# Cross attention beside the feed-forward products: tiles' scores every three slots, values two slots later, output products and third norms three slots later

## The chip, the core and the metric

The kernel runs on one core of a Trainium2 chip. The core has five engines, each with a queue of its own that it works off in order: TensorE (PE; its weight loads are shown apart as PEld), VectorE (DVE), ScalarE (ACT), GpSimd (POOL) and SyncE (SP), which here issues the DMAs. Engines wait for each other through semaphores. Matmuls write into eight banks of PSUM, from which VectorE and ScalarE read. The metric is the device time of one execution in microseconds (us); several executions are timed, and one more is recorded by the profiler.

## The reference

A transformer of one encoder layer (77 rows of context, two sequences) and one decoder layer (2 x 2048 rows, width 512, 16 heads of 32, feed-forward width 2048), in float32. Biases of scores depend on the relative position only. The decoder's part:

```python
y = y + _mha(yn, yn, dec_sa_in_w, dec_sa_in_b, dec_sa_out_w, dec_sa_out_b, sb)
y = y + _mha(_ln(y, dec_n2_s, dec_n2_b), memory, dec_ca_in_w, dec_ca_in_b, dec_ca_out_w, dec_ca_out_b, cb)
h = _ln(y, dec_n3_s, dec_n3_b)
y = y + (jax.nn.relu(h @ dec_ff1_w.T + dec_ff1_b) @ dec_ff2_w.T + dec_ff2_b)
```

`_mha` projects queries from its first argument and keys and values from its second, takes softmax(q k / sqrt(32) + bias) times v by heads, and multiplies by the output weights. In the cross attention (`ca`) the keys are the 77 rows that the encoder made, so each query row has 16 x 77 probabilities.

## The kernel before

The 4096 decoder rows are eight blocks of 512 rows (`blocks`), each of four tiles of 128 rows. The encoder, the self attention of all blocks and the cross attention of the first block come first. The last part, lines 2000 to 2006, is the one around the change: for each block x it runs the feed-forward part of block x in `per` = 56 slots, and beside it the cross attention of block x + 1, which `cross` (line 1747) deals out over the same slots.

A slot is `next(side)`, which issues all functions of `cross` planned for that slot, and then `ff_slot` (line 1724). Instructions go to each engine in exactly this order: the schedule is written by hand. Large products are built in Strassen's manner (Winograd's form): seven products of sums of quarters instead of eight. Hence the sums on VectorE and GpSimd and the lists `ONE` and `TWO` of which product uses which sums.

**Feed-forward slots.** Slots 0 to 27 (`first_product`, line 1649; matmuls at line 1658): hidden = first weights times norm, twice seven products in two slots each. The result goes out of PSUM by a copy on ScalarE (L1668), by an add on VectorE (L1671), by both ReLU activations on ScalarE (L1674), or by several of these, depending on the product. Products accumulate in banks 4 to 7, so a product waits until what is read from its bank has been read. Slots 28 to 55 (`second_product`, line 1678; matmuls at line 1687): seven products of seven parts each; a product takes four slots with 2, 2, 2 and 1 parts. Results are mixed at L1695 to L1703 and added to the rows at L1707 on GpSimd. The left operands of product j are sums made by `sums_h` (line 1615) in slots 24 + 4j to 27 + 4j: half sums on VectorE (L1607) and quarter sums at L1625 and, through the helper `minus`, L965, on VectorE and GpSimd. For j = 0 they are a sum on VectorE in slot 24, one on GpSimd in slot 25, one on VectorE in slot 26, one on GpSimd in slot 27; part 2 of the product, the first of slot 29, multiplies the one of slot 25.

**Side slots.** Per block and tile t:

- slots 0 to 7: second norm (`norm_stages`, line 785: statistics, centering, turning by TensorE with activations at L814); slots 11 to 14 add a row on GpSimd (L806);
- slots 9 to 12: queries (`q_product`, matmuls L1773);
- `SCORE_AT[t]` + 0, 2, 3, 3, 6: scores (L839; then L848 and L849 on VectorE, which take maxima from PSUM and subtract them, with an added bias at L846 for two tiles of the one block that starts the second sequence), exponential on ScalarE (L852), sums and reciprocal on VectorE (L857, L858), normalizing on GpSimd (L863), turning of 32 x 32 blocks on VectorE (`blocks_turned`, L1804). The scores of one tile fill all of banks 0 to 3;
- `VALUES_AT` + g, g = 0 to 3: probabilities times values (`times_v`, matmuls L1815) into banks 0 to 3, for all four tiles at once, so the first of them needs all four turned tiles. With the last group, `values_out` (line 1823) copies the results out (L1827) and makes sums of them for the output products (L965, L1833);
- `OUT_AT`: two sets of seven output products (`o_product`, matmuls L1854), four slots each, added to the rows at L1858;
- `NORM_AT[t]` + 0, 2, 4: the third norm, of which the turned tile goes to `nTt`. The feed-forward part of the next block reads it from its slot 0 on (sums of it on GpSimd in slots 0, 1, 4 and 6, L965).

Functions planned for one slot are issued in the order in which `cross` appended them, for the tiles by t: turning of an earlier tile, then sums and normalizing of the next one, then scores of the one after.

Weights come in tiles of 256 KB through a ring of places. `weight_tiles` (line 1532) lists them in the order of use: in each slot first those of the side stage (`cross_tiles`, line 1521, which follows `Q_SLOTS` and `O_SLOTS`), then those of the feed-forward product. `feed` (line 1559) is called in each slot and issues as many loads on SP as places have come free.

Of the kernel before, what the change touches and what calls it, by code (L numbers as in the profile page):

```python
# [54 lines left out]
def tile_encoder_decoder(ctx: ExitStack, tc: tile.TileContext, ins, out):  # L55
# [103 lines left out]
    with (  # L159
# [625 lines left out]
        def norm_stages(y, n, row, place, done):  # L785

            keep = {}

            def stats():
                st = sm.tile([P, 6], F32, name="bnst", tag="bnst")  # L790
                mv = sm.tile([P, 2], F32, name="cmv", tag="cmv", bufs=4)
                rs = sm.tile([P, 3], F32, name="crs", tag="crs", bufs=4)
                nc.vector.bn_stats(st, y())
                nc.vector.bn_aggr(mv, st)
                nc.vector.tensor_scalar_add(rs[:, 0:1], mv[:, 1:2], EPS)
                nc.gpsimd.tensor_tensor(rs[:, 1:2], rs[:, 0:1], mhalf[:, 0:1], ALU.pow)
                nc.gpsimd.tensor_scalar(rs[:, 2:3], mv[:, 0:1], rs[:, 1:2], -1.0, ALU.mult, ALU.mult)
                keep.update(rs=rs)

            def center():  # L800
                xn = keep["xn"] = place()
                rs = keep["rs"]
                nc.scalar.activation(xn, y(), AF.Identity, bias=rs[:, 2:3], scale=rs[:, 1:2])

            def add():
                nc.gpsimd.tensor_tensor(y(), y(), row, ALU.add)  # L806

            def turned():
                xn, pt, dst = keep["xn"], bank(), done()
                for c in range(NC):  # L810
                    nc.tensor.transpose(pt[:, ts(c, P)], xn[:, ts(c, P)], ident)  # L811
                for c in range(NC):
                    sc, bi = vec(f"dec_{n}_s", c), vec(f"dec_{n}_b", c)
                    nc.scalar.activation(dst[:, c, :], pt[:, ts(c, P)], AF.Identity, bias=bi, scale=sc)  # L814

            return stats, center, turned, add
# [543 lines left out]
        def y_of(x, t):  # L1360
            return ys[x % 3][:, t, :]
# [150 lines left out]
            return ins["dec_ff1_wT"][c * TOK : (c + 1) * TOK, o : o + TOK].rearrange("(c p) o -> p c o", p=P)  # L1512

        Q_SLOTS = {9: (0, 1), 10: (2, 3), 11: (4, 5), 12: (6,)}
        SCORE_AT = (13, 17, 21, 25)
        VALUES_AT = 32
        OUT_AT = (37, 41)
        NORM_AT = (41, 42, 45, 46)
        O_SLOTS = {at + k: js for at in OUT_AT for k, js in enumerate(((0, 1), (2, 3), (4, 5), (6,)))}

        def cross_tiles(n):
# [225 lines left out]
        def cross(x):  # L1747
# [58 lines left out]
            def times_v(g):  # L1806
                if g == 0:
                    for _ in range(P // RB):
                        bank()
                pT = prs.rearrange("p t (h c q) -> p t h c q", h=H, c=KC)  # L1810
                for c in range(KC):
                    for a in range(P // RB):
                        for r in range(HC):
                            h = g * HC + r
                            nc.tensor.matmul(  # L1815
                                psum[rows4(r), a, ts(g, P)], v4[ts(a, RB), c, ts(h, HD)],
                                pT[ts(a, RB), :, h, c, :], start=(c == 0), stop=(c == KC - 1),
                            )
# [24 lines left out]
            def o_product(t, j):  # L1843
                if j == 0:
                    held["out"] = bank(), bank()
                name, by, chain, fresh, to = ONE[j]
                a, mm = of_o(t, name), held["out"][chain][:, :TOK]
                if by[0] == "T":
                    w = next_w(2)
                else:  # L1850
                    r, c = int(by[0]) - 1, int(by[1]) - 1
                    w = wbt[:, 2 * r : 2 * r + 2, ts(c, TOK)]
                for c in range(2):
                    nc.tensor.matmul(  # L1854
                        mm, a[:, ts(c, P)], w[:, c, :], start=fresh and c == 0, stop=c == 1, skip_group_check=True
                    )
                d = y_of(x, t + int(to[0]) - 1)[:, ts(int(to[1]) - 1, TOK)]
                ve.tensor_tensor(d, d, mm, ALU.add)  # L1858
# [3 lines left out]
            for n, js in O_SLOTS.items():  # L1862
                t = 0 if n < OUT_AT[1] else 2
                plan[n].append(lambda t=t, js=js: [o_product(t, j) for j in js])
# [12 lines left out]
            for g in range(NC):  # L1877
                plan[VALUES_AT + g].append(lambda g=g: times_v(g))
            plan[VALUES_AT + NC - 1].append(values_out)
            for t in range(TB):  # L1880
                at = SCORE_AT[t]
                y = lambda t=t: y_of(x, t)
# [7 lines left out]
                fs = norm_stages(y, "n3", bo, next_xt, lambda t=t: nTt[:, :, ts(t, P)])  # L1890
                at = NORM_AT[t]
                for k, f in zip((0, 2, 4), fs):
# [151 lines left out]
```

## Time and profile before

| | us |
|---|---|
| runs (3): median, lowest, highest | 2768.71, 2766.49, 2769.78 |
| profiled execution, its own time | 2766.32 |
| its span, first to last instruction | 2764.5 |
| TensorE busy | 2685.6 |
| VectorE busy | 1906.8 |
| ScalarE busy | 1474.9 |
| GpSimd busy | 997.9 |

The last part of the kernel, in which the slots of eight blocks run, lies between about 1680 and 2764 us of the span; one block of 56 slots with its side stage takes 142 us. Views of the profile that follow: the head of the page (span; busy time, share and instructions of each engine); the list of waits (who waited for whom: total us, times, longest us); the timeline (start in us, duration, engine, line and operation, output and inputs, count; in brackets the idle time before it and what ended it); and windows (from:to, length, busy time and count of PE, PEld, DVE, ACT and POOL, then the granted TensorE clock as a share of full speed, the busy share of the DMA engines, and GB/s). Rows of the timeline that stand one behind another are merged instructions of one line; matmuls are pipelined, and their ends are modelled, so ends can overlap the next start.

### The profile page before, as it was taken

The page shows a single profiled execution, that of the slowest core. Times are in us where ns is not written, and L with a number is a line of the kernel's source. Part 1 is how long each engine was busy: PE and PEld are TensorE (multiplying, and loading weights), DVE is VectorE, ACT ScalarE, POOL GpSimd, SP SyncE. Part 2 cuts the span into 40 slices and gives each one's busy share as a digit, 9 for nine tenths or more (in the row PEclk, how much of TensorE's full clock was granted, in tenths as well). Part 3 has the DMA queues.
Part 4 walks back from the last instruction along what each step waited for, and adds up shares of the span by engine and source line. Part 5 has one row for each costly group of instructions (what it writes and reads, how often), then busy time and mean ns, then how long its engine had stood idle before and what let it go on. Part 6 is the DMA issues. An engine that isn't in the chain of part 4 may idle for free.

```text
span 2764.5 us, 70789 instructions
## 1 busy us (share of the span) xinstructions
PE 2685.6 (97%) x27950; PEld 2192.0 (79%) x27950; DVE 1906.8 (69%) x5473; ACT 1474.9 (53%) x2866; POOL 997.9 (36%) x845
## 2 busy tenths in 40 slices
PE   9999999999999999999999999898989898989898
PEld 5678777787776677777787787888879797979798
DVE  4776688888884677778888874747474747474745
ACT  3555567777886566667777774242414242424231
POOL 2612145401201404223200112645454555555445
PEclk9999999999999999999999999999999999999999
DMA  8734355411215413333211234666657565657476
GB/s 238 214 90 143 118 167 171 137 52 44 74 33 124 128 57 94 110 115 127 87 52 38 67 111 152 195 182 187 188 179 225 158 209 163 214 158 218 135 228 206
DMA packets 296893, 386.20 MB, mean 140 GB/s; under 512 B 41330, under 2 KB 165794, under 8 KB 296434
## 3 DMA queue, kind: packets, MB, share of 16 engines
q1 hardware_dynamic: 296562, 381.68, 46.2%
q8 instruction: 221, 3.62, 0.6%
q14 instruction: 110, 0.90, 0.1%
HBM read 335.10 MB, written 46.47 MB: 138 GB/s over the span
## 4 chain that ended last, share of the span: by engine, by line
PE 83%; DVE 10%; ACT 3%; issue 2%; POOL 1%; DMA 1%; SPq 0%; DVEq 0%; ACTq 0%; POOLq 0%
PE psum L427 18%; PE psum L375 11%; PE psum L1687 10%; PE psum L1658 9%; PE psum L456 9%; PE psum L1137 8%; PE psum L1773 3%; PE psum L1854 3%; PE psum L1052 2%; PE psum L1815 2%; DVE pp L849 1%; DVE cmx L848 1%; DVE csu L857 1%; PE psum L590 1%; PE psum L811 1%
## 5 line engine op out<-in xcount | busy, mean ns | idle before, releaser
L406 ACT ACTIVATE pp<-pp,nm 128x128 f32<-128x128 f32 (+15 forms) x512 | 611.8, 1200 | 29.4 <-DVE nm L401 28.6
L384 DVE TENSOR_SCALAR_CACHE_REDUCE pp<-psum 128x512 f32<-128x512 f32 (+3 forms) x1024 | 556.1, 590 | 51.2 <-PE psum L375 49.7
L434 ACT COPY pts<-psum 128x512 f32<-128x512 f32 x714 | 384.1, 594 | 311.2 <-PE psum L427 263.3
L427 PE MATMUL psum<-ident,pp 128*128 128x128 f32 x4352 | 527.4, 276 | 4.6 <-ACT nT L310 4.0
L427 PEld LDWEIGHTS psum<-ident,pp 128*128 128x128 f32 x4352 | 471.3, 141 | 55.1 <-DVE pp L384 21.6
L375 PE MATMUL psum<-kT,q 32*128 32x512 f32 (+3 forms) x2560 | 336.8, 559 | 4.1 <-ACT kT L231 1.4
L456 PEld LDWEIGHTS psum<-pts,vv 128*32 128x32 f32 x8704 | 226.4, 110 | 127.3 <-DVE pp L384 55.4
L432 DVE COPY pts<-psum 128x512 f32<-128x512 f32 x374 | 245.2, 686 | 81.5 <-PE psum L427 79.3
L456 PE MATMUL psum<-pts,vv 128*32 128x128 f32 x8704 | 279.4, 275 | 0.7 <-DVE mx L391 0.3
L965 POOL TENSOR_TENSOR pp<-pp 128x512 f32<-128x512 f32 x159 | 206.8, 1321 | 107.4 <-DMA pp<-in_dec_ff_wT_dram 50.9
L375 PEld LDWEIGHTS psum<-kT,q 32*128 32x128 f32 x2560 | 146.5, 184 | 109.0 <-issue 41.1
L391 DVE CUSTOM_DVE_ANT_0 pp<-psum,bias 128x256 f32<-128x256 f32 (+1 forms) x512 | 195.9, 411 | 19.7 <-PE psum L375 19.7
L1687 PE MATMUL psum<-oT,pp 128*128 128x128 f32 x1544 | 193.6, 280 | 0.4 <-POOL pp L965 0.4
L1687 PEld LDWEIGHTS psum<-oT,pp 128*128 128x128 f32 x1544 | 186.3, 195 | 6.2 <-issue 3.5
L1674 ACT ACTIVATE kT<-kT,vecs 128x256 f32<-128x256 f32 x192 | 87.1, 500 | 194.9 <-DVE kT L1671 194.2
L1695 ACT COPY pts<-psum 128x128 f32<-128x128 f32 x56 | 15.1, 269 | 307.9 <-PE psum L1687 307.9
L863 POOL TENSOR_TENSOR pp<-pp,cri 128x1232 f32<-128x1232 f32 x32 | 75.6, 2363 | 272.9 <-DVE cri L858 248.7
L1671 DVE TENSOR_TENSOR kT<-kT,psum 128x512 f32<-128x512 f32 x96 | 65.4, 681 | 153.9 <-PE psum L1658 153.7
L494 POOL TENSOR_TENSOR oT<-rirows,oT 128x512 f32<-128x512 f32 x30 | 38.4, 1278 | 294.9 <-DMA rirows<-rec 169.4
L1658 PE MATMUL psum<-vv,oT 128*128 128x256 f32 x600 | 138.2, 381 | 0.0
L1687 PE MATMUL psum<-pp 128*128 128x128 f32 x1016 | 132.4, 284 | 1.8 <-POOL pp L965 1.2
L1687 PEld LDWEIGHTS psum<-pp 128*128 128x128 f32 x1016 | 126.1, 199 | 6.8 <-issue 2.7
(287 smaller groups left out, 4583.4 us busy)
## 6 DMA issues: line engine op xcount, KB each, us to landing
oT<-w_d SPq DMA_DIRECT2D x311, 256.0 KB
pp<-w_d SPq DMA_DIRECT2D x209, 256.0 KB
bias<-tzg SPq DMA_DIRECT2D x128, 128.0 KB
pp<-in_dec_ff_wT_dram SPq DMA_DIRECT2D x63, 256.0 KB
wqk<-in_dec_sa_in_wT_dram SPq DMA_DIRECT2D x52, 256.0 KB
oT<-in_dec_ff_wT_dram SPq DMA_DIRECT2D x49, 256.0 KB
wqk<-sa_q SPq DMA_DIRECT2D x84, 128.0 KB
oT<-wo_d SPq DMA_DIRECT2D x34, 256.0 KB
```

What stands on the lines that cost most here:

```text
L375: nc.tensor.matmul(banks[r][:, : kn * P], q[rows4(r), ts(t, P)], kT[rows4(r), g, k0 * P : (k0 + kn) * P], start=True, stop=True,)
L384: nc.vector.tensor_scalar(p[:, k0 : k0 + far], s[:, :far], 1.0, None, ALU.mult, ALU.max, accum_out=st["mx"][:, r, c : c + 1],)
L391: nc.vector.tensor_tensor_reduce(p[:, k0 + far : i + 1], s[:, far:kn], near[:, 2 - (kn - far) :], 1.0, LOWEST, ALU.add, ALU.max, accum_out ...
L406: nc.scalar.activation(p, p, AF.Exp, bias=nm, accum_out=to)
L427: nc.tensor.transpose(pt[:, ts(x, P)], state[n]["p"][r][:, k], ident)
L432: nc.vector.tensor_copy(pts[:, : len(load), :], pt[:, :w])
L434: nc.scalar.copy(pts[:, : len(load), :], pt[:, :w])
L456: nc.tensor.matmul(ot[rows4(r)], vv[:, k, ts(g * HC + r, HD)], got.pop((n, k, r)), start=k == k0 and (whole or not begun), stop=k == k1 - ...
L965: engine.tensor_tensor(out, a, b, ALU.subtract)
L1137: nc.tensor.matmul(mm[:, ts(f, TOK)], left[:, c, ts(f, P)], right[:, c, :], start=c == 0, stop=c == 1,)
L1658: nc.tensor.matmul(mm[:, ts(f, TOK)], a[:, c, ts(f, P)], b[:, c, :], start=fresh and f == 0 and c == 0, stop=c == 1, skip_group_check=True,)
L1687: nc.tensor.matmul(psum[:, bank_i, ts(col, P)], lhs[:, c, :], w[:, c, :], start=fresh and k in (0, 3) and c == 0, stop=c == 3, skip_group_ ...
```

## The change

Four constants change, and with them, through `O_SLOTS`, the slots of the output products and the place of their weight tiles in the order of loads.

```diff
-        SCORE_AT = (13, 17, 21, 25)
-        VALUES_AT = 32
-        OUT_AT = (37, 41)
-        NORM_AT = (41, 42, 45, 46)
+        SCORE_AT = (13, 16, 19, 22)
+        VALUES_AT = 34
+        OUT_AT = (40, 44)
+        NORM_AT = (44, 45, 48, 49)
         O_SLOTS = {at + k: js for at in OUT_AT for k, js in enumerate(((0, 1), (2, 3), (4, 5), (6,)))}
```

The slots of the side stage in both versions:

| | before | after |
|---|---|---|
| scores of tiles 0 to 3 | 13, 17, 21, 25 | 13, 16, 19, 22 |
| exponentials | 15, 19, 23, 27 | 15, 18, 21, 24 |
| sums, normalizing | 16, 20, 24, 28 | 16, 19, 22, 25 |
| blocks turned | 19, 23, 27, 31 | 19, 22, 25, 28 |
| values | 32 to 35 | 34 to 37 |
| output products | 37 to 40, 41 to 44 | 40 to 43, 44 to 47 |
| third norm, first and last step | 41, 42, 45, 46 and 45, 46, 49, 50 | 44, 45, 48, 49 and 48, 49, 52, 53 |

## The prediction

> **What bounds the kernel now.** I read the head of the page, then TensorE's waits in the stretch from 1600 to 2764 us (seven blocks of 56 slots in which a side stage, the cross attention of the next block, runs between the feed-forward products of this one), then the timelines of one block on TensorE and VectorE, then the granted clock.
>
> ```profile
> span 2764.5 us, 70789 instructions
> PE 2685.6 (97%) x27950; PEld 2192.0 (79%) x27950; DVE 1906.8 (69%) x5473; ACT 1474.9 (53%) x2866; POOL 997.9 (36%) x845
> ```
> ```profile
> PE psum L1815 <- DVE pp L1804: 42.7, 7, 7.9
> PE psum L1854 <- DVE pts L1833: 9.1, 7, 1.3
> PE psum L1854 <- DVE vv L1858: 3.4, 7, 0.5
> ```
>
> TensorE is the bound (97% of the span), and in this stretch it waits at three places only, once per block each: 42.7 us for the last turned tile of probabilities (L1804) ahead of the first value product (L1815), 9.1 us for the sums of the values (L1833) ahead of the output product (L1854), 3.4 us inside that product. Here is one block on TensorE (start, duration, count, idle time before):
>
> ```profile
> 2274.92 1.13 PE L839 MATMUL psum<-pts,bias 32*128 32x77 f32 x32
> ...
> 2277.81 5.34 PE L1658 MATMUL psum<-nT,oT 128*128 128x256 f32 x24
> ...
> 2311.12 1.06 PE L1687 MATMUL psum<-oT,kT 128*128 128x128 f32 x8
> 2317.99 2.17 PE L1815 MATMUL psum<-pp,pts 32*32 32x128 f32 x96 [5.81 <-DVE pp L1804]
> 2320.09 3.78 PE L1687 MATMUL psum<-oT,pp 128*128 128x128 f32 x16
> 2323.80 1.56 PE L1815 MATMUL psum<-pp,pts 32*32 32x128 f32 x96
> 2325.29 2.05 PE L1687 MATMUL psum<-pp 128*128 128x128 f32 x16
> ```
>
> I count time from 2274.92, where the first tile's scores start in slot 13. A score costs 1.06 to 1.1, a slot of first products 1.73 (5.34 for three, ends overlapping), a slot of second products of 16 matmuls 1.78 and of 8 matmuls 0.89. Slots 13 to 31 are four scores, 15 first-product slots and one set of four second-product slots (6.24): 36.4. TensorE is through with them at 37.3 (2312.18), so it has lost 0.9 in all on the way, and then stands still for 5.81.
>
> Behind that stall the same work takes longer: 2.17 for a value group that takes 1.56 two rows on, 3.78 for products that take 2.05. The clock says why:
>
> ```profile
> 1740.50:1746.30 5.80, 0.02 (x1) 0.00 (x0) 5.80 (x6) 0.00 (x0) 5.10 (x4) 0.78 0.90 314
> 2595.30:2601.10 5.80, 0.09 (x1) 0.00 (x0) 5.80 (x6) 0.00 (x0) 5.10 (x4) 0.95 0.43 154
> 2312.20:2317.20 5.00, 0.00 (x0) 0.00 (x0) 5.00 (x5) 0.00 (x0) 4.30 (x3) 1.00 1.01 358
> 2170.40:2176.20 5.80, 0.00 (x0) 0.00 (x0) 5.80 (x6) 0.00 (x0) 5.10 (x4) 0.50 0.53 201
> 1746.30:1753.30 7.00, 6.98 (x212) 6.00 (x213) 4.65 (x6) 0.00 (x0) 6.22 (x5) 0.70 0.30 91
> 2601.10:2608.10 7.00, 6.91 (x186) 6.03 (x192) 4.72 (x7) 0.00 (x0) 6.23 (x5) 0.56 0.13 41
> ```
>
> The third figure from the right is the granted clock. It falls to 0.50 during each of the seven stalls and stays there for a while. The last two rows are the first and last of the seven 7 us behind a stall; their shortfall, 7 x (1 - clock) over all seven, sums to 17.6 us: 2.5 per block. So the stall and what hangs on it cost 42.7 + 17.6, the two smaller waits 12.5. The block that reads bias tiles (it scores from 2129.10) comes to its stall 2.0 later than the others do. Together 74.8 us can be won at most.
>
> What holds TensorE is VectorE's queue:
>
> ```profile
> 2276.07 0.48 DVE L848 TENSOR_REDUCE cmx<-psum 128x4 f32<-128x308 f32 x1 [3.80 <-PE psum L839]
> ...
> 2279.29 0.48 DVE L849 TENSOR_TENSOR pp<-psum,cmx 128x308 f32<-128x308 f32 x1
> 2281.50 1.44 DVE L857 TENSOR_REDUCE csu<-pp 128x16 f32<-128x1232 f32 x1 [1.74 <-ACT pp L852]
> ...
> 2283.19 0.69 DVE L1671 TENSOR_TENSOR kT<-kT,psum 128x512 f32<-128x512 f32 x1
> ...
> 2287.85 0.68 DVE L1671 TENSOR_TENSOR kT<-kT,psum 128x512 f32<-128x512 f32 x1
> 2288.44 1.77 DVE L1804 STREAM_TRANSPOSE pp<-pp 128x1536 f32<-128x1536 f32 x1
> ...
> 2310.68 3.89 DVE L1607 TENSOR_TENSOR pp<-kT 128x512 f32<-128x512 f32 x3
> ...
> 2316.17 1.76 DVE L1804 STREAM_TRANSPOSE pp<-pp 128x1536 f32<-128x1536 f32 x1
> ```
>
> Per tile: scores S 3.6 to 3.7, sums U 1.65 (L857, L858), turn X 1.7, and for the products an add of 0.6 (L1671, start to start 0.59). Tile t's are S0 to S3 and so on. The last turn X3 stands behind four half sums (L1607) of the second products.
>
> **The change, part by part.** No instruction is added or removed. Scores move 0, 1, 2, 3 slots earlier, values and their turns' deadline 2 later, output products 3 later. The other rows that the new queue needs:
>
> ```profile
> 2288.56 0.91 ACT L1674 ACTIVATE kT<-kT,vecs 128x256 f32<-128x256 f32 x2 [3.74 <-DVE kT L1671]
> 2289.84 1.25 ACT L852 ACTIVATE pp<-pp 128x1232 f32<-128x1232 f32 x1
> ```
> ```profile
> 2301.32 2.27 POOL L863 TENSOR_TENSOR pp<-pp,cri 128x1232 f32<-128x1232 f32 x1 [6.06 <-DVE cri L858]
> 2303.54 1.26 POOL L965 TENSOR_TENSOR pp<-pp,kT 128x512 f32<-128x512 f32 x1
> ```
>
> VectorE's new order, with ends: S0 4.85; U0 waits for its exponential as now, 8.3; S1 (slot 16) 11.9; adds of slots 16 and 17, 13.1; X0 14.8; exponential 1 stands on ScalarE behind the two activations that wait for the adds (0.9 each, then 1.25), so it ends at 15.5, and U1 at 17.2; S2 (slot 19) 20.8; X1 22.5; U2 24.1; S3 27.7; adds of 22 and 23, half sum (0.55), add of 24: 30.1; X2 31.8; U3 33.4. Then GpSimd: normalizing tile 3 (L863, N3) to 35.9, and the next sum (L965) to 37.2.
>
> That last step is the new wait. N3 moves from slot 28 to slot 25, where the side stage's functions are issued ahead of the feed-forward ones. So it passes the sums that the first second-product takes from GpSimd (issued in slots 25 and 27), which now queue behind it. TensorE's slot 29 multiplies the first of them.
>
> TensorE: tile 3's scores come at 19.1 in slot 22 and need all four banks, which S2 frees at 20.8: wait 1.7. Slot 29 comes at 32.0 + 0.7 (most of its lag as now) + 1.7 = 34.4 and waits to 37.2: 2.8. After that slot 32 begins at 41.7; its second left operand is the fourth half sum, behind N3 (35.9), X3 (1.7), two half sums (1.3 and 0.7 to 1.3), one more (1.3), a short add and itself (1.3): 42.5 to 43.1, needed at 42.6. Values in slot 34, at 45.3, find X3 done since 37.6. So 4.5 of new waits per block, 31.5 in seven, and 4.3 more in the block with bias tiles, by the same walk with its longer scores, worked out from these rows:
>
> ```profile
> 2130.24 0.48 DVE L846 TENSOR_TENSOR pp<-psum,pp 128x308 f32<-128x308 f32 x1 [3.80 <-PE psum L839]
> ...
> 2135.52 0.48 DVE L849 TENSOR_TENSOR pp<-pp,cmx 128x308 f32<-128x308 f32 x1
> ```
>
> Together 35.8. The outputs and the norms:
>
> ```profile
> 2333.85 0.42 DVE L965 TENSOR_TENSOR wqk<-xr,psum 128x256 f32<-128x256 f32 x1 [6.05 <-ACT pts L1827]
> ...
> 2335.77 0.41 DVE L1833 TENSOR_TENSOR pts<-psum,pts 128x256 f32<-128x256 f32 x1
> 2371.72 1.50 ACT L814 ACTIVATE nT<-psum,vecs 128x128 f32<-128x128 f32 x4 [0.57 <-PE psum L811]
> 2383.91 1.27 POOL L965 TENSOR_TENSOR vv<-nT 128x512 f32<-128x512 f32 x1
> ```
>
> From the last value group (ends 2332.2) to the end of its sums (2336.2) are 4.0. TensorE has 2.67 of products for that now and 4.45 after (slots 37 to 39), so the 9.1 go; the 3.4 sit behind half sums that meet the product elsewhere, and I count them gone (if not, 3 us less). The third norm's last activations end at 2373.2, their first reader on GpSimd starts at 2383.9; three slots later takes at most 4.5 of these 10.7, so this costs nothing. Eight weight tiles of the output product enter SP's queue three slots later, in the order in which they are used; no wait above is for a DMA, so I price that at nothing, at worst a few tenths per block.
>
> Left is the clock after the new waits. By the seven stalls it halved 2.1 to 5.3 us after TensorE went idle (a row of length L and clock c halved 2 x L x (1 - c) before its end: 3.2 and 5.2 for the first and the last of the seven, which are quoted; in the 0.50 row idle time began at 2168.34, so 2.1; in the 5.00 us row not yet). That looks like fixed windows, each judged at its end by its idle share. A wait of 1.7 is shorter than any of these. For 2.8, four of the seven phases (2.1, 2.9, 3.0, 3.2 us) would have halved it, three (5.0 to 5.3) not. I take four, and one more for the bias block's longer waits, at 2.5 each as now: 12.5. Bounds: none, or all nine: 0 to 22.5.
>
> Sum: 74.8 - 35.8 - 12.5 = 26.5 us less. The profiled execution took 2766.3; the median shown, 2768.7, is 2.4 above it, and 2768.7 - 26.5 = 2742.
>
> **Rivals.** (a) The clock needs a whole idle window to fall, so no new wait costs clock: 39.0 less, 2730. The Trainium skill, "TensorE: Matmul & The Clock Gate", Part 1, has this rule: half clock after at least one idle window of about 3.4 us. By that rule 2.8 us could never do it; the trace speaks against it, with 0.50 granted 2.1 us after idle time began. Chance 0.20.
> (b) No new wait arises: VectorE's lag is smaller than worked out, or the sums come in time. All 74.8 go but for the score waits (up to 12): about 2700. Against it: VectorE has the same work and idles only some 2.6 in the new order up to U3. Chance 0.08.
> (c) Both new waits cost clock in every block, 16 x 2.5 = 40: nothing is left, 2768 to 2770. Against it: 1.7 is under the shortest 2.1. Chance 0.07.
> (d) Slower: exponentials late on ScalarE. Each stands behind activations that wait for VectorE's adds; if U1, U2 and U3 each idle 1.8 as U0 does, the sum behind N3 comes 4.6 later. It decides from 3.8 later (26.5 / 7). Price: 39.0 - 7 x 4.6 - 10 x 2.5 = 18 us longer, 2787. Against it: U2 and U3 find VectorE behind, not ahead. Chance 0.05.
>
> **How the numbers follow.** My forecast has 0.60; its own range is no cold clock with VectorE 1 us per block earlier (2722) to all nine with 1 us later (2759). It contains (a). (b), (c), (d) and a little of the edges lie outside: range 2720 to 2758. A measurement of this kernel can tell 0.2%, 5.5 us, from no change. Faster by more: forecast, (a), (b) and a bit of (c), 0.90; within, the rest of (c), 0.05; slower, (d), 0.05.
>
> **What would show it.** Right: no wait of L1815 for L1804; per block a wait of L839 for L849 of about 1.7 and one of L1687 for GpSimd's L965 (behind L863) of about 2.8, in slot 29; no wait of L1854 for L1833; granted clock under 1 behind some of the waits, not all. Wrong: the wait of L1687 absent, or longer than 4, or new waits at the start of a block (first readers of the third norm).

## The result and the profile after

| | before | after |
|---|---|---|
| median of 20 runs (us) | 2768.49 | 2761.84 |
| lowest and highest | 2763.96, 2771.78 | 2754.05, 2770.9 |
| profiled execution, its own time | 2766.32 | 2757.55 |
| its span | 2764.5 | 2755.8 |

The ratio is 0.9975, with a 95% interval of 0.9966 to 0.9984: faster by a quarter of a per cent, 6.65 us. Forecast were 26.5 us and 2742, with a range of 2720 to 2758. The direction was right; the time lies above the range.

TensorE's waits in the seven blocks of the changed kernel (who waited for whom, total us, times, longest), 1600 to 2755 us of the span:

```profile
PE psum L1687 <- POOL pp L965: 23.7, 9, 3.2
PE psum L1815 <- issue: 8.1, 8, 1.9
PE psum L839 <- DVE pp L849: 2.8, 6, 0.5
PE psum L839 <- DVE pp L846: 2.0, 2, 1.0
PE psum L1687 <- issue: 1.9, 2, 1.3
PE psum L1854 <- DVE vv L1858: 1.1, 7, 0.2
```

The 42.7 us of L1815 for L1804 and the 9.1 of L1854 for L1833 are gone. In their place stands the forecast wait of L1687 for GpSimd's L965, and one that was not forecast: 10 us "issue", in which the profile shows nothing that TensorE waits for. Here is the same block as in the prediction, TensorE's timeline from its first score at 2270.41:

```profile
2289.72 0.91 PE L839 MATMUL psum<-pts,bias 32*128 32x77 f32 x6
2291.09 1.11 PE L839 MATMUL psum<-pts,bias 32*128 32x77 f32 x26 [0.46 <-DVE pp L849]
...
2307.69 1.16 PE L1687 MATMUL psum<-pp 128*128 128x128 f32 x8 [3.15 <-POOL pp L965]
2308.68 4.47 PE L1687 MATMUL psum<-oT,pp 128*128 128x128 f32 x24
...
2317.55 1.49 PE L1815 MATMUL psum<-pp,pts 32*32 32x128 f32 x96
2318.97 2.05 PE L1687 MATMUL psum<-pp 128*128 128x128 f32 x16
2320.95 1.49 PE L1815 MATMUL psum<-pp,pts 32*32 32x128 f32 x96
2322.36 0.49 PE L1687 MATMUL psum<-oT,pp 128*128 128x128 f32 x2
2324.19 0.83 PE L1687 MATMUL psum<-oT,pp 128*128 128x128 f32 x6 [1.33 <-issue]
```

Tile 3's scores take 2.41 instead of 1.06 (2289.72 to 2292.13), slot 29 waits 3.15, 24 matmuls behind it take 4.47 instead of 2.84, and in slot 35 TensorE stops after two of eight matmuls of one weight tile, whose operands are all there. The windows (busy times, then granted clock, busy share of the DMA engines, GB/s) put the clock and the DMA engines beside this; first two of the changed kernel, then two of the kernel before around its old stall:

```profile
2309.13:2312.54 3.41, 3.41 (x18) 3.41 (x18) 3.28 (x5) 0.02 (x1) 2.25 (x2) 0.52 0.56 178
2317.60:2322.40 4.80, 4.80 (x210) 4.08 (x209) 2.90 (x4) 0.00 (x0) 4.03 (x4) 1.00 1.02 337
```
```profile
2312.20:2318.00 5.80, 0.01 (x2) 0.01 (x2) 5.80 (x6) 0.00 (x0) 5.10 (x4) 0.93 0.94 334
2318.00:2324.00 6.00, 6.00 (x128) 5.22 (x144) 4.63 (x6) 0.00 (x0) 5.22 (x5) 0.50 0.08 28
```

Before, the DMA engines did their backlog (0.94) while TensorE stood still, and were nearly idle (0.08) when the value products began. After, the value products begin while they are full (1.02). It is alike in all seven blocks: in the first 6 us of value products the DMA engines are busy 0.08 to 0.22 before and 0.73 to 1.00 after.

### The profile page after: what moved, and what is told of

Its sections match the earlier page's. It is cut to its first block, busy times and chain, and to the rows that moved or that the text cites. A ratio compares the mean times of both kernels' runs of the same rounds, so it can differ in the third digit from the quotient of the medians.

```text
span 2755.8 us, 70838 instructions
## 1 busy us (share of the span) xinstructions
PE 2696.6 (98%) x27950; PEld 2198.3 (80%) x27950; DVE 1918.2 (70%) x5473; ACT 1473.2 (53%) x2866; POOL 1005.9 (37%) x845
## 3 DMA queue, kind: packets, MB, share of 16 engines
q8 instruction: 221, 3.62, 0.5%
## 4 chain that ended last, share of the span: by engine, by line
PE 82%; DVE 8%; issue 3%; ACT 3%; POOL 2%; DMA 1%; SPq 1%; DVEq 0%; POOLq 0%; ACTq 0%
PE psum L427 18%; PE psum L1687 11%; PE psum L375 11%; PE psum L456 9%; PE psum L1658 9%; PE psum L1137 8%; PE psum L1773 3%; PE psum L1854 3%; PE psum L1052 2%; PE psum L1815 2%; DVE csu L857 1%; DVE pp L849 1%; DVE cmx L848 1%; PE psum L811 1%; ACT pp L406 1%
## 5 line engine op out<-in xcount | busy, mean ns | idle before, releaser
L965 POOL TENSOR_TENSOR pp<-pp 128x512 f32<-128x512 f32 x159 | 212.1, 1357 | 111.7 <-DMA pp<-in_dec_ff_wT_dram 50.8
L1687 PE MATMUL psum<-oT,pp 128*128 128x128 f32 x1544 | 199.1, 284 | 18.2 <-POOL pp L965 16.2
L1687 PEld LDWEIGHTS psum<-oT,pp 128*128 128x128 f32 x1544 | 190.8, 199 | 25.2 <-POOL pp L965 17.4
L1687 PE MATMUL psum<-pp 128*128 128x128 f32 x1016 | 128.3, 280 | 7.7 <-POOL pp L965 7.5
L1687 PEld LDWEIGHTS psum<-pp 128*128 128x128 f32 x1016 | 123.1, 195 | 11.6 <-POOL pp L965 8.2
```

The lines of the kernel that those rows point to most:

```text
L965: engine.tensor_tensor(out, a, b, ALU.subtract)
L1687: nc.tensor.matmul(psum[:, bank_i, ts(col, P)], lhs[:, c, :], w[:, c, :], start=fresh and k in (0, 3) and c == 0, stop=c == 3, skip_group_ ...
```

## The experiments

e1 to e4, e5 to e8, and e9 with e10 ran on three chips. Each time is a median, and each ratio is to the kernel before on the same chip (medians 2766.55, 2767.67 and 2768.60), so medians of different groups may be some 2 us apart for that alone.

| run | edit against | us | ratio (95%) |
|---|---|---|---|
| the change | before | 2761.84 | 0.9975 (0.9966 to 0.9984) |
| e1 | the change: tile 3's normalizing back in slot 28 | 2733.15 | 0.9876 (0.9863 to 0.9889) |
| e2 | the change: idle time of slot 29 filled | 2750.53 | 0.9944 (0.9932 to 0.9956) |
| e3 | the change: rows loaded in slots 16 to 19 | 2750.49 | 0.9938 (0.9927 to 0.9950) |
| e4 | the change: old slots of scores | 2737.47 | 0.9895 (0.9882 to 0.9908) |
| e5 | the change: only its slots of scores | 2764.74 | 0.9989 (0.9978 to 0.9999) |
| e6 | e1 and e3 together | 2720.24 | 0.9827 (0.9814 to 0.9841) |
| e7 | e4 and e3 together | 2734.43 | 0.9879 (0.9866 to 0.9893) |
| e8 | e6, fourth tile's scores in slot 23 | 2720.80 | 0.9827 (0.9813 to 0.9840) |
| e9 | e6 and four idle copies of 256 KB in slots 28 to 31 | 2734.13 | 0.9880 (0.9866 to 0.9895) |
| e10 | e6 and eight such copies | 2758.29 | 0.9967 (0.9953 to 0.9981) |

The theory at the start: what is left sits in the wait behind tile 3's normalizing and in the clock behind that wait. The rival: the DMA engines, which had caught up during the old stall, are now the limit, and give back whatever is freed.

**e1, the order on GpSimd.**

```diff
-                for k, f in zip((0, 2, 3, 3, 6), fs):
+                for k, f in zip((0, 2, 3, 6, 9) if t == 3 else (0, 2, 3, 3, 6), fs):
```

> The changed kernel with only tile 3's normalizing (L863) in slot 28 and its turn (L1804) in slot 31, as before the change, so that GpSimd's sums of slots 25 and 27 stand ahead of it. If what is left is the wait of L1687 for GpSimd (22 us in seven blocks) and the cold clock behind it (7 x 1.7 = 12): 2728 to 2738, no wait of L1687 for L965 on GpSimd over 0.5. If the DMA engines are the limit there (they are at 1.0 from slot 32 on, and TensorE stops inside value products for nothing the profile shows): the time comes back as longer stops in L1815 and L1687, 2750 to 2760.

Measured 2733.15, inside the first range. In its list of waits (1680 to 2680 us) the one for GpSimd is gone, and the unnamed ones have grown:

```profile
PE psum L1815 <- issue: 12.1, 9, 2.7
PE psum L839 <- DVE pp L849: 4.5, 10, 0.7
PE psum L839 <- DVE pp L846: 2.0, 2, 1.0
PE psum L1687 <- DVE pp L965: 1.5, 6, 0.3
```

So the first theory holds for some 27 to 29 us (28.7 by medians, 26.8 with each kernel against its own kernel before), and the rival for a rest.

**e2, the clock.** 24 transposes, not read by anyone, stand ahead of slot 29's products.

```diff
+            if x + 1 < len(blocks) and (j, part) == (0, 1):
+                for _ in range(24):
+                    nc.tensor.transpose(psum[:, 0, :P], ident, ident)
```

> The changed kernel with 24 transposes of the identity into bank 0 (about 2.6 us, their result is not read) ahead of the products of slot 29, in the time in which TensorE waits for GpSimd. If the clock falls by the idle share of a window, the idle time of 0.6 left cannot lower it: granted clock 1.00 behind slot 29 in all seven blocks, 7 x 1.7 = 12 us less than the changed kernel, 2748 to 2753. If the stops for the DMA engines take the place, as TensorE is then earlier at slot 32: 2757 to 2762.

Measured 2750.53, 11.3 less than the changed kernel by medians, 9.4 less with each against its own kernel before. In its timeline (line numbers three higher here) the transposes take 2.8 of the idle time; the window row below it has the clock at 1.00, and it does not fall behind slot 29 in any of the seven blocks:

```profile
2308.62 2.78 PE L1685 MATMUL psum<-ident 128*128 128x128 f32 x24
2311.95 1.16 PE L1690 MATMUL psum<-pp 128*128 128x128 f32 x8 [0.54 <-POOL pp L965]
```
```profile
2311.40:2318.00 6.60, 6.06 (x55) 6.06 (x55) 6.52 (x10) 0.27 (x1) 5.22 (x5) 1.00 0.58 157
```

Work that does nothing shortened the kernel. The halved clock behind slot 29 is thereby shown as a cost of its own.

**e3, the traffic in slots 28 to 31.**

```diff
-            if FIRST <= n < FIRST + TB:
-                new_y(x + 2, n - FIRST)
+            if 16 <= n < 16 + TB:
+                new_y(x + 2, n - 16)
```

> The changed kernel with the loads of the next rows (4 x 256 KB, new_y) issued in slots 16 to 19 instead of 28 to 31. If TensorE's stops inside the value products (10 us in seven blocks, for nothing the profile shows) come from full DMA engines, they shrink to under 3 and the time falls by 5 to 8, to 2754 to 2757. If they are TensorE's own limit on short matmuls, they stay at 8 to 10 and the time at 2760 to 2763.

Measured 2750.49, more than expected (11.35 less than the changed kernel); the stops in the value products fell as expected, those of L1687 hardly:

```profile
PE psum L1687 <- POOL pp L965: 22.1, 7, 3.2
PE psum L839 <- DVE pp L849: 3.6, 8, 0.5
PE psum L1815 <- issue: 2.5, 6, 0.8
PE psum L839 <- DVE pp L846: 2.0, 2, 1.0
PE psum L1687 <- issue: 1.7, 2, 1.2
```

Between the two profiled executions the difference is 7.1 (2757.55 and 2750.49); the rest is that the changed kernel's profiled run lay 4.3 under its median, and e3's at its own.

**e4 and e5, one half of the change each.** e4 has the old `SCORE_AT` with the new `VALUES_AT`, `OUT_AT` and `NORM_AT`, e5 the reverse.

> The old slots of scores (13, 17, 21, 25) with the new ones of values, outputs and norms. Worked out from the old trace: the wait ahead of the values (5.8) becomes one of 3.1 in slot 32 for VectorE's fourth half sum (L1607, done at 41.3 after the first score, needed at 38.2), the waits for L1833 and L1858 (12.5) go, the clock falls in four to seven blocks. If the earlier scores brought little and the later values and outputs the gain: 2755 to 2763, as the changed kernel or better. If the earlier scores matter: 2764 to 2768.

> The new slots of scores (13, 16, 19, 22) with the old ones of values, outputs and norms. By the traces so far: the wait ahead of the values (5.8 and its clock) goes, the waits of L1839 for banks, of L1687 for the sum behind tile 3's normalizing (3.1) and its clock come, and the 9 to 12 us ahead of and in the output products stay: 2758 to 2766. If the earlier scores are what shortened the changed kernel: 2750 to 2756.

(L1839 there stands for L839.) Measured 2737.47 and 2764.74. e4 beats the changed kernel by far, which was not expected. The wait in slot 32 came nearly as worked out (2.5 for 3.1), unnamed in the profile, but TensorE goes on as soon as the third of VectorE's half sums is through (2298.05), not the fourth:

```profile
2298.15 3.56 PE L1687 MATMUL psum<-oT,pp 128*128 128x128 f32 x16 [2.49 <-issue]
```
```profile
2294.15 3.90 DVE L1607 TENSOR_TENSOR pp<-kT 128x512 f32<-128x512 f32 x3
```

The gain is that e4 stops only 3.0 us in value products and has not the scores' wait for banks; its wait in slot 32 stands in place of the 3.15 in slot 29. In e5 the 22.1 for GpSimd stands beside the 9.1 for L1833, as expected:

```profile
PE psum L1687 <- POOL pp L965: 22.1, 7, 3.2
PE psum L1854 <- DVE pts L1833: 9.1, 7, 1.3
```

So the later values and outputs alone are worth 29 us, the earlier scores alone 3, both together 6.65: the earlier scores, as they were placed, take 22 back.

**e6, e7, e8.** e6 joins e1 and e3, e7 joins e4 and e3. Tile 3 is normalized in slot 28 and turned in slot 31 in both, so they differ in the slots of the scores and of what hangs on them (exponentials, sums, the first three tiles' normalizing and turns).

> Both at once: tile 3's normalizing behind the sums (2733 by itself) and the rows loaded in slots 16 to 19. In the former run TensorE stopped 12 us inside value products for nothing the profile shows, with full DMA engines. If that is the cause there too, 8 to 12 less: 2721 to 2726. If the rows were late for another reason, 2731 to 2735.

> Old slots of scores, new ones of values, outputs and norms (2737 by itself), and the rows loaded in slots 16 to 19. That kernel stopped only some 3 us inside value products, so 0 to 4 less: 2733 to 2738. A gain of 8 or more as in the changed kernel would say that the loads in slots 28 to 31 cost something beside those stops.

> As e6, with the fourth tile's scores in slot 23, its sums in 26, its normalizing in 28 and turn in 31. The scores of slot 22 lose 1.3 per block waiting for banks that VectorE still reads (TensorE is there at 19.3, VectorE through at 20.6); one slot later they find them free: 7 to 9 less than e6, 2712 to 2718. If VectorE, not the bank, sets the end, the time comes back ahead of slot 32 and it stays within 2 of e6.

Measured 2720.24, 2734.43 and 2720.80, e7 within its first range, e6 a little under it, while e8 went the way of its rival: the wait for banks is gone and comes back, as waits for half sums ahead of slot 32 (5.8 of the 7.2 unnamed in L1687, and 3.5 for L1607). e6 is 14.2 faster than e7: earlier scores do help once nothing is put ahead of the sums of slots 25 and 27. e6 is the fastest of all, 47.4 us under the 2767.67 of the kernel before on its chip.

**What the unnamed stops are.** They stand in the middle of groups whose operands are there. Their places tell more. These are rows of the first three blocks of the changed kernel:

```profile
1755.60 0.47 PE L1815 MATMUL psum<-pp,pts 32*32 32x128 f32 x20 [1.88 <-issue]
...
1896.76 0.92 PE L1815 MATMUL psum<-pp,pts 32*32 32x128 f32 x46 [1.42 <-issue]
...
2036.75 1.29 PE L1815 MATMUL psum<-pp,pts 32*32 32x128 f32 x73 [0.68 <-issue]
2037.97 1.16 PE L1687 MATMUL psum<-pp 128*128 128x128 f32 x8
2039.06 0.92 PE L1815 MATMUL psum<-pp,pts 32*32 32x128 f32 x47
2040.50 0.94 PE L1815 MATMUL psum<-pp,pts 32*32 32x128 f32 x49 [0.52 <-issue]
```

Between the two stops of the third block lie 73 + 8 + 47 = 128 matmuls, each with its weight load: 256 instructions. In e2, the first three blocks' stops moved by exactly the transposes put in ahead of them: where 20, 46 and 73 matmuls of a group were left, there are 20 + 24 = 44, 46 + 48 = 94, and 73 + 72 - 128 = 17:

```profile
1758.83 0.89 PE L1818 MATMUL psum<-pp,pts 32*32 32x128 f32 x44 [2.24 <-issue]
1899.57 1.47 PE L1818 MATMUL psum<-pp,pts 32*32 32x128 f32 x94 [1.17 <-issue]
2041.14 0.46 PE L1818 MATMUL psum<-pp,pts 32*32 32x128 f32 x17 [2.09 <-issue]
```

So TensorE stops at places of its own instruction stream that lie 256 apart. The other runs agree: counted in matmuls from the program's start, modulo 128, the stops of the seven blocks lie at 58, 24, 117, 83, 48, 14 and 107, within one, in the changed kernel and all runs but e5 (one to three off). The page has a queue that fits that stream (q8: 3.62 MB in 221 packets, 16.4 KB each; 221 x 256 is 56576, against 2 x 27950 matmuls and weight loads). Its packets are in the trace. The stop at 2324.19 that is shown above began at 2322.86; here are the DMA queues from 2321.50 to 2323.00 (packets, MB, share of the 16 engines' time):

```profile
q1 hardware_dynamic: 240, 0.45, 93.8%
q8 instruction: 1, 0.02, 4.2%
```

That one packet lasts from 2321.72 to 2322.73, and TensorE goes on 1.46 later. So it is each time: from 1680 us on, all 93 such stops of 0.15 us and more in the kernels' twelve traces end 1.2 to 1.6 us after a packet of this queue has ended, while for the waits for half sums in e4, e7 and e8 this distance scatters between 1.6 and 20. The packets themselves take 0.9 to 1.7 us, about 1.0 in the middle, with or without a stop: the instructions come late because their packet starts late, not because it takes long. The Trainium skill, "Runtime: NRT & Kernel Launch", Instruction fetch mechanics, says that instructions are refilled in blocks of 16 KiB, 256 instructions, and that this is mostly hidden; the block size agrees, the hiding does not hold here. The last two runs put traffic alone back into e6. (The copies are not quite the rows' traffic, as they end in the device memory and not in the core's own.)

```diff
+            if x + 2 < len(blocks) and FIRST <= n < FIRST + TB:
+                b, m = blocks[x + 2]
+                nc.sync.dma_start(spare_d[:, n - FIRST, :], y1[b][m][:, n - FIRST, :])
```

> e6 (2720) with four copies of 256 KB from one place of the device memory to another in slots 28 to 31 of each block but two; nobody reads them. They put back the traffic that the rows had there, and nothing else. If TensorE's stops in the value products come from its next 256 instructions (128 matmuls with their weight loads: in three blocks of the changed kernel two stops stand exactly that far apart) coming late through full DMA engines, stops in L1815 rise from 3 to 7 to 12 and the time to 2727 to 2734. If it was the rows themselves (their place, who waits for them), 2719 to 2723.

> As e9 with eight such copies. With the DMA engines as the cause the stops and the time grow further, to 2735 to 2750, with waits for weight tiles beside them; else 2719 to 2723.

Measured 2734.13 (at the upper edge of what was expected) and 2758.29 (above it, and with no wait for a weight tile named in its list). The stops in the value products of e6, e9 and e10 (L1815; L1819 and L1820 in the latter two):

```profile
PE psum L1815 <- issue: 2.7, 5, 0.8
```
```profile
PE psum L1819 <- issue: 11.7, 8, 2.4
```
```profile
PE psum L1820 <- issue: 21.0, 12, 4.6
```

The stops grow with the traffic: 2.7, 11.7, 21.0. The time grows by more, 13.9 and 38.1, since the clock falls behind such stops too: five and six times in these two profiles, and never in e6's. Two more falls, in all three, stand at the scores of the block with bias tiles.

## Why the prediction was wrong

**The steps that held.** VectorE's queue was worked out nearly to the tenth: the sum behind tile 3's normalizing was to end 37.2 after the first score, and TensorE went on at 37.28 (2307.69). The wait in slot 29 was to be 2.8 and is 3.15; the scores' wait in slot 22, 1.7, costs 1.35. Values were to begin at 45.3; they begin at 47.14 in this block, where the clock cost 1.7. The waits of L1854 went, but for 1.1 of 12.5. The later norms cost nothing: no wait stands at the start of a block.

**The step that failed** is the one about the DMAs: "no wait above is for a DMA, so I price that at nothing, at worst a few tenths per block". That was read from the list of waits of a kernel in which the 5.8 us stall itself was the cover. During it the DMA engines worked off the weight tiles and the rows, and they were nearly idle when the value products called for instructions. The stall went, and with it the cover: value products, 256 instructions in some 4 us against 14 among second products alone, now ran into full engines. The stage from the first to the last value product took 11.9 to 14.3 us in the seven blocks, 12.98 on the mean, where e4 shows 10.8 in its two blocks without a stop and 11.8 on the mean. The 10.0 us of stops in the list were priced at nothing, or some 2 at worst. Where the traffic was moved away (e3) the time is 2750.49: inside the range, and still 8 above the forecast.

**A size that was off:** the clock. Five falls at 2.5 were counted, 12.5. Behind slot 29 it fell in six blocks of seven; each cost 1.7, since it came back after 3.4 us rather than 6.8 (the 0.52 row above is one such stretch). The block with bias tiles lost 3.4 more at its scores, and the first block 1.7 behind a stop. Together 15.4. Of rival (a), a whole idle window, nothing is left: 3.15 us of waiting never fill 3.41. The falls of the clock in this trace lie whole multiples of 3.413 us apart, so the windows are fixed, as the prediction took them to be. A window's idle share is not all that decides. Of these four windows of the changed kernel the first halved the clock, the next two, of the first block, did not, and the last, in the first block's value products, did:

```profile
2305.60:2309.02 3.42, 1.33 (x12) 1.33 (x12) 3.42 (x3) 1.02 (x4) 3.31 (x3) 1.00 0.56 183
1735.58:1738.99 3.41, 1.97 (x17) 1.75 (x15) 3.38 (x4) 1.85 (x5) 2.22 (x1) 1.00 0.73 219
1738.99:1742.40 3.41, 1.63 (x14) 1.63 (x15) 3.41 (x3) 0.77 (x3) 3.00 (x3) 1.00 0.47 156
1752.64:1756.06 3.42, 1.54 (x97) 0.97 (x65) 0.00 (x0) 0.00 (x0) 3.34 (x4) 1.00 0.78 285
```

Among products of 128 rows, 2.09 idle of 3.41 lowered it and 1.44 and 1.78 did not, nor did 1.85 in the kernel before (1880.25 to 1883.67); in e4 1.74 did (2571.02 to 2574.44), so the limit, somewhere above half a window, is not sharp by these readings. In value products 1.88 lowered it, and 1.35 in e9 (1885.92 to 1889.33); at the scores of the block with bias tiles 0.92 did in e6 (2133.77 to 2137.18). So small matmuls seem to count for less than large ones; no run tested that by itself.

**The sum.** Of the 26.5 forecast, the profiled runs show 8.8. The stops (10.0), the clock (2.9 more than counted) and L1858 (1.1) make 14.0 of the 17.7 missing. The new waits took some 33.3 (22.1 in slot 29, 11.2 at the scores) of the 35.8 counted, so about 6 us are not assigned. The medians are 6.65 apart, since the changed kernel's profiled run lay 4.3 under its median and the other 2.2.

**The other rivals.** (b) needed the sums in time; e1 made them so and came to 2733, not 2700; with most of the stops gone as well (e6) it is 2720. (c) came near the measured time for another reason: the clock cost 15, not 40. (d) did not occur.

## What to carry to other kernels

A long stall is also a time in which transfers catch up, so that what follows, its instructions too, finds the DMA engines free. Before a stall is costed as pure gain, look at the DMA share during it and behind it, and ask what the next stage does if it starts with that backlog. And a step that is moved earlier goes ahead of what now stands there on every queue: here a normalizing that was off TensorE's path got in front of two small sums that were on it.

## What the runs showed of the hardware

- TensorE can stop where 256 instructions of its stream end, when the DMA engines are full, and the profile gives no releaser for it. All 93 such stops end 1.2 to 1.6 us after a packet of the instruction queue; the shift by 24, 48 and 72 in e2 and the growth with traffic in e9 and e10 show it too.
- The granted clock halves at the end of a window of 3.413 us on a fixed grid. Among matmuls of 128 rows it did so with 2.09 us idle, and not with 1.78 or 1.85 (the kernel before, 1880.25 to 1883.67), but with 1.74 in e4, so idle time by the profile gives no sharp limit; where value products or scores stood in the window, less was enough (0.92 in e6). 24 useless transposes in such a gap were worth 9 to 11 us.
- Twenty executions of the changed kernel lie between 2754 and 2771 us, with a mean clock of 0.993 and 0.994 in the two shortest and 0.987 to 0.989 in the three longest. That the phase of the windows does this is likely, but no run tested it.
